# Batch-norm of pairwise outer products: statistics from 39x39 moment tables, W read from PSUM, and a tile loop split over three engines in a fixed order

## Chip, cores and metric

One core of one Trainium2 chip. The metric is device time in microseconds (us) of one launch. All runs below are fast-state runs. TensorE (PE) works only in the statistics (its last matmul ends at 102 us in the kernel before). The engines are called PE, DVE (VectorE), ACT (ScalarE), POOL (GpSimd) and SP (SyncE), as in the profile.

## The reference

Inputs xi and xj are 1024 x 39 x 16, f32. For each of the 741 pairs of fields (r, c) with c < r it forms the 16x16 outer product of xj[r] and xi[c], normalises it with the mean and variance of that pair over batch and both 16s, applies gamma and beta, and multiplies by a 16x16 matrix W.

```python
rows, cols = np.tril_indices(39, k=-1)                      # 741 pairs
cross = xj[:, rows, :, None] * xi[:, cols, None, :]         # 1024 x 741 x 16 x 16
mean = jnp.mean(cross, axis=(0, 2, 3), keepdims=True)
var = jnp.mean(jnp.square(cross - mean), axis=(0, 2, 3), keepdims=True)
normed = (cross - mean) * jax.lax.rsqrt(var + BN_EPS)
normed = normed * gamma[None, :, None, None] + beta[None, :, None, None]
out = normed[:, :, None, :, :] * W[None, None, :, :, :]
return jnp.transpose(out, (0, 2, 1, 3, 4))                  # 1024 x 1 x 741 x 16 x 16, 777 MB
```

So 5 MB are read and 777 MB written. Folded, it is (xj * (xi * s) + t) * W with one s and one t per pair.

## The kernel before

The batch is on the partitions, 8 samples on each. After the statistics, a loop goes over the rows r and over groups of nt samples. For each tile: POOL scales xi by s (xs), ACT forms the 16 products per sample (DVE those of rows up to 6), DVE does one fused (y + t) * W per pair, in place, and one store takes the tile out.

```python
rows = ctx.enter_context(tc.tile_pool(name="rows", bufs=4))
scaled = ctx.enter_context(tc.tile_pool(name="scaled", bufs=2))
for r in order:                                   # short and long rows in turn
    n0 = first[r]
    nt = max(n for n in (1, 2, 4, 8) if NT % n == 0 and (n == 1 or n * r < F))
    for t0 in range(0, NT, nt):
        xs = scaled.tile([P, nt, r, E], F32, tag="xs", ...)
        nc.gpsimd.tensor_tensor(xs, xi_sb[:, t0 : t0 + nt, 0:r, :],
            s_sb[:, :, n0 : n0 + r, :].to_broadcast([P, nt, r, E]), ALU.mult)          # L166
        y = rows.tile([P, nt, r, E, E], F32, tag="y", ...)
        for t in range(nt):
            # ... r <= 6: one nc.vector.tensor_tensor for all products (L175), else:
            for i in range(E):
                nc.scalar.activation(y[:, t, :, i, :], xs[:, t], AF.Copy,
                                     scale=xj_sb[:, t0 + t, r, i : i + 1])             # L183
        y2 = y.rearrange("p t n i j -> p t n (i j)")
        for c in range(r):
            nc.vector.scalar_tensor_tensor(y2[:, :, c, :], y2[:, :, c, :],
                t_sb[:, n0 + c : n0 + c + 1], w_sb.to_broadcast([P, nt, EE]),
                ALU.add, ALU.mult)                                                     # L191
        nc.sync.dma_start(out_v[:, t0 : t0 + nt, n0 * EE : (n0 + r) * EE], ...)
```

The statistics (cut) build 741-wide pair products on DVE and POOL (L100), average them over the batch with 128 matmuls against ones (L111), and finish with 741-wide steps.

Of the kernel before, what the change touches and what calls it, by code (L numbers as in the profile page):

```python
# [7 lines left out]
F32 = mybir.dt.float32  # L8
AF = mybir.ActivationFunctionType
ALU = mybir.AluOpType  # L10
AX = mybir.AxisListType

BN_EPS = 1e-5
# Rows of at most this many pairs have their outer products on VectorE, the longer ones on ScalarE.
VECTOR_ROW = 6


@with_exitstack
def tile_pair_outer_batchnorm(
# [9 lines left out]
    """out[b, 0, (r, c), i, j] = (xj[b, r, i] * xi[b, c, j] * s[r, c] + t[r, c]) * W[i, j] for c < r,  # L29
    with s = gamma * rsqrt(var + eps) and t = beta - mean * s.  # L30

    The batch lies on the partitions, b = p * NT + t. Mean and variance of a pair need only the
    mean and the variance over E of each field: with a = xj[b, r], b = xi[b, c],
      mean_ij(a_i b_j)           = A B
      mean_ij((a_i b_j - m) ** 2) = (A B - m) ** 2 + (A ** 2 + va) vb + va B ** 2
    (A, B the means and va, vb the variances of a and b), and only positive terms are summed.
    """
# [6 lines left out]
    H0 = (NP + 1) // 2  # L44
    halves = ((0, H0), (H0, NP))
# [6 lines left out]
    s_sb = cpool.tile([P, 1, NP, 1], F32, name="s_sb")  # L52
    t_sb = cpool.tile([P, NP], F32, name="t_sb")
# [10 lines left out]
    with tc.tile_pool(name="stat", bufs=1) as st, tc.tile_pool(  # L64
        name="dev", bufs=2
    ) as devp, tc.tile_pool(name="ps", bufs=1, space=bass.MemoryType.PSUM) as psp:
        g_sb = st.tile([P, NP], F32, name="g_sb")
        b_sb = st.tile([P, NP], F32, name="b_sb")
        nc.gpsimd.dma_start(w_sb[:, 0, :], w.rearrange("o i j -> (o i j)").partition_broadcast(P))
        nc.gpsimd.dma_start(g_sb, gamma.partition_broadcast(P))  # L70
        nc.gpsimd.dma_start(b_sb, beta.partition_broadcast(P))
        ones = st.tile([P, P], F32, name="ones")
        nc.gpsimd.memset(ones, 1.0 / NB)

        # mean and variance over E of each field, per sample
        ma = st.tile([P, NT, F, 1], F32, name="ma")
        mb = st.tile([P, NT, F, 1], F32, name="mb")
        va = st.tile([P, NT, F, 1], F32, name="va")
        vb = st.tile([P, NT, F, 1], F32, name="vb")
        for t0 in range(0, NT, TS):  # L80
            for x, m, v in ((xj_sb, ma, va), (xi_sb, mb, vb)):
                xs, ms, vs = x[:, t0 : t0 + TS], m[:, t0 : t0 + TS], v[:, t0 : t0 + TS]
                nc.vector.tensor_reduce(ms[:, :, :, 0], xs, AX.X, ALU.add)  # L83
                nc.vector.tensor_scalar_mul(ms, ms, 1.0 / E)
                dev = devp.tile([P, TS, F, E], F32, tag="dev", name="dev")
                nc.vector.tensor_tensor(dev, xs, ms.to_broadcast([P, TS, F, E]), ALU.subtract)  # L86
                nc.scalar.activation(dev, dev, AF.Square)  # L87
                nc.vector.tensor_reduce(vs[:, :, :, 0], dev, AX.X, ALU.add)  # L88
                nc.vector.tensor_scalar_mul(vs, vs, 1.0 / E)
        ma, mb, va, vb = (x[:, :, :, 0] for x in (ma, mb, va, vb))  # L90
        sa = st.tile([P, NT, F], F32, name="sa")
        sb = st.tile([P, NT, F], F32, name="sb")
        nc.vector.tensor_mul(sb, mb, mb)  # L93
        nc.vector.tensor_mul(sa, ma, ma)
        nc.vector.tensor_add(sa, sa, va)

        def pairs(engine, rows, cols, name):
            q = st.tile([P, NT, NP], F32, name=name)
            for r in range(1, F):
                engine.tensor_tensor(  # L100
                    q[:, :, first[r] : first[r] + r],
                    rows[:, :, r : r + 1].to_broadcast([P, NT, r]),
                    cols[:, :, 0:r],
                    ALU.mult,
                )
            return q

        def batch_mean(ps, qs, start, stop):
            for k, (q, t) in enumerate((q, t) for q in qs for t in range(NT)):
                for acc, (n0, n1) in zip(ps, halves):  # L110
                    nc.tensor.matmul(  # L111
                        acc[:, : n1 - n0],
                        ones,
                        q[:, t, n0:n1],
                        start=start and k == 0,
                        stop=stop and k == len(qs) * NT - 1,
                    )

        # mean over the batch, on every partition
        q_c = pairs(nc.gpsimd, va, sb, "q_c")  # L120
        q_a = pairs(nc.vector, ma, mb, "q_a")
        ps_m = [psp.tile([P, 512], F32, name=f"ps_m{h}") for h in range(2)]
        ps_v = [psp.tile([P, 512], F32, name=f"ps_v{h}") for h in range(2)]
        batch_mean(ps_m, [q_a], True, True)
        q_b = pairs(nc.vector, sa, vb, "q_b")
        batch_mean(ps_v, [q_b, q_c], True, False)
        mean = st.tile([P, 1, NP], F32, name="mean")
        for acc, (n0, n1) in zip(ps_m, halves):
            nc.scalar.copy(mean[:, 0, n0:n1], acc[:, : n1 - n0])  # L129
        for t in range(NT):  # L130
            nc.vector.tensor_sub(q_a[:, t], q_a[:, t], mean[:, 0])  # L131
            nc.scalar.activation(q_a[:, t], q_a[:, t], AF.Square)  # L132
        batch_mean(ps_v, [q_a], False, True)

        # rstd = 1 / sqrt(var + eps), with a Newton step behind the table's square root
        var = st.tile([P, NP], F32, name="var")
        for acc, (n0, n1) in zip(ps_v, halves):
            nc.vector.tensor_scalar_add(var[:, n0:n1], acc[:, : n1 - n0], BN_EPS)  # L138
        inv = st.tile([P, NP], F32, name="inv")
        nc.vector.reciprocal(inv, var)  # L140
        rstd = st.tile([P, NP], F32, name="rstd")
        nc.scalar.activation(rstd, inv, AF.Sqrt)  # L142
        nc.vector.tensor_mul(inv, var, rstd)
        nc.vector.tensor_mul(inv, inv, rstd)  # L144
        nc.vector.tensor_scalar(inv, inv, -0.5, 1.5, ALU.mult, ALU.add)
        nc.vector.tensor_mul(rstd, rstd, inv)  # L146

        s2 = s_sb[:, 0, :, 0]
        nc.vector.tensor_mul(s2, rstd, g_sb)
        nc.vector.tensor_mul(t_sb, mean[:, 0], s2)  # L150
        nc.vector.tensor_sub(t_sb, b_sb, t_sb)

    # short and long rows in turn, so that VectorE and ScalarE share the outer products evenly
    order = []
    for k in range(1, (F - 1) // 2 + 1):
        order += [k, F - k]
    assert sorted(order) == list(range(1, F))

    rows = ctx.enter_context(tc.tile_pool(name="rows", bufs=4))
    scaled = ctx.enter_context(tc.tile_pool(name="scaled", bufs=2))  # L160
    for r in order:
        n0 = first[r]
        nt = max(n for n in (1, 2, 4, 8) if NT % n == 0 and (n == 1 or n * r < F))
        for t0 in range(0, NT, nt):
            xs = scaled.tile([P, nt, r, E], F32, tag="xs", name=f"xs_{r}_{t0}")
            nc.gpsimd.tensor_tensor(  # L166
                xs,
                xi_sb[:, t0 : t0 + nt, 0:r, :],
                s_sb[:, :, n0 : n0 + r, :].to_broadcast([P, nt, r, E]),
                ALU.mult,  # L170
            )
            y = rows.tile([P, nt, r, E, E], F32, tag="y", name=f"y_{r}_{t0}")
            for t in range(nt):
                if r <= VECTOR_ROW:
                    nc.vector.tensor_tensor(  # L175
                        y[:, t],
                        xs[:, t].unsqueeze(2).to_broadcast([P, r, E, E]),
                        xj_sb[:, t0 + t, r : r + 1, :].unsqueeze(3).to_broadcast([P, r, E, E]),
                        ALU.mult,
                    )  # L180
                else:
                    for i in range(E):
                        nc.scalar.activation(  # L183
                            y[:, t, :, i, :],
                            xs[:, t],
                            AF.Copy,
                            scale=xj_sb[:, t0 + t, r, i : i + 1],
                        )
            y2 = y.rearrange("p t n i j -> p t n (i j)")
            for c in range(r):  # L190
                nc.vector.scalar_tensor_tensor(  # L191
                    y2[:, :, c, :],
# [38 lines left out]
```

## Time and profile before

| | before |
|---|---|
| time, median | 3103.07 us (3102.97 to 3104.05, 3 runs) |
| DVE / ACT / POOL busy | 79% / 65% / 54% |
| share of the 16 DMA engines' time | 59% |
| statistics end (first scaling of the loop) | 112.5 us |

From the page of the kernel before, the three groups of the loop: line, engine, operation, tiles, a shape, count, then busy us, mean ns of one, and the idle time just before them with what ended most of it.

```profile
L191 DVE SCALAR_TENSOR_TENSOR y<-y,t_sb,w_sb 128x256 f32<-128x256 f32 (+2 forms) x5068 | 2314.6, 534 | 610.3 <-ACT y L183 610.1
L183 ACT ACTIVATE y<-xs,xj_sb 128x608 f32<-128x608 f32 (+31 forms) x4096 | 1994.9, 580 | 978.7 <-POOL xs L166 978.7
L166 POOL TENSOR_TENSOR xs<-xi_sb,s_sb 128x576 f32<-128x576 f32 (+19 forms) x206 | 1637.3, 7958 | 1368.8 <-ACT y L183 1315.6
```

The odd number is the 7958 ns in the third line: the same engine does a multiply of 352 elements in 0.79 us elsewhere in this trace.

### The profile page before, as it was taken

What the parts mean: (1) busy time and instruction counts of PE and PEld (TensorE: products, weight loads), DVE (VectorE), ACT (ScalarE), POOL (GpSimd) and SP (SyncE); (2) the same over time, 40 slices, a digit from 0 to 9 for tenths busy, and PEclk for the clock granted to TensorE, in tenths of its full rate; (3) what the DMA queues carried; (4) which work ended last, traced back from release to release, by engine and by line L of the source; (5) the groups of instructions that cost most, each with busy time, mean ns of one, the idle gap of its engine ahead of it and who ended that gap; (6) DMA issues with size and microseconds to landing.
All of it is one profiled execution on the core that took longest, in us unless ns stands there. A gap on an engine that the chain in (4) does not pass through costs nothing.

```text
span 3100.0 us, 10969 instructions
## 1 busy us (share of the span) xinstructions
PE 45.6 (1%) x128; PEld 26.7 (1%) x128; DVE 2448.0 (79%) x5253; ACT 2015.7 (65%) x4117; POOL 1659.1 (54%) x252
## 2 busy tenths in 40 slices
PE   2300000000000000000000000000000000000000
PEld 1100000000000000000000000000000000000000
DVE  8687888888888787777777787768777777778786
ACT  2446455464635777777676767676868686868685
POOL 2375757665666656555646464646363636362623
PEclk9655555555555555555555555555555555555555
DMA  2165656566555656666656656565656565666666
GB/s 78 78 265 228 282 244 259 250 269 271 250 252 248 293 237 281 256 268 268 288 249 263 265 240 272 246 281 242 270 243 281 244 281 249 276 263 268 275 267 275
DMA packets 43653, 783.71 MB, mean 253 GB/s; under 512 B 3472, under 2 KB 4496, under 8 KB 11824
## 3 DMA queue, kind: packets, MB, share of 16 engines
q1 hardware_dynamic: 42784, 779.56, 59.1%
q10 hardware_dynamic: 576, 2.56, 0.2%
q0 software_dynamic: 208, 0.89, 0.1%
q14 instruction: 84, 0.69, 0.1%
q8 instruction: 1, 0.02, 0.0%
HBM read 6.00 MB, written 776.99 MB: 253 GB/s over the span
## 4 chain that ended last, share of the span: by engine, by line
ACT 48%; POOL 45%; DVE 3%; issue 2%; PE 1%; DMA 0%; POOLq 0%; DVEq 0%; ACTq 0%
ACT y L183 48%; POOL xs L166 45%; PE ps_v L111 1%; DVE y L191 1%; DVE q_a L100 1%; DVE dev L86 0%; PE ps_m L111 0%; DMA xj_sb<-in_r_xj_dram 0%; DVE ma L83 0%; DVE vb L88 0%; DVE va L88 0%; DVE mb L83 0%; DVE inv L140 0%; DVE rstd L146 0%; DVE inv L144 0%
## 5 line engine op out<-in xcount | busy, mean ns | idle before, releaser
L191 DVE SCALAR_TENSOR_TENSOR y<-y,t_sb,w_sb 128x256 f32<-128x256 f32 (+2 forms) x5068 | 2314.6, 534 | 610.3 <-ACT y L183 610.1
L183 ACT ACTIVATE y<-xs,xj_sb 128x608 f32<-128x608 f32 (+31 forms) x4096 | 1994.9, 580 | 978.7 <-POOL xs L166 978.7
L166 POOL TENSOR_TENSOR xs<-xi_sb,s_sb 128x576 f32<-128x576 f32 (+19 forms) x206 | 1637.3, 7958 | 1368.8 <-ACT y L183 1315.6
L175 DVE TENSOR_TENSOR y<-xs,xj_sb 128x256 f32<-128x256 f32 (+5 forms) x48 | 51.5, 1136 | 1.5 <-POOL xs L166 1.4
L100 POOL TENSOR_TENSOR q_c<-va,sb 128x8 f32<-128x8 f32 (+37 forms) x38 | 19.6, 553 | 39.3 <-DVE sb L93 39.3
L87 ACT ACTIVATE dev<-dev 128x1248 f32<-128x1248 f32 x8 | 9.9, 1243 | 26.1 <-DVE dev L86 25.9
L129 ACT COPY mean<-ps_m 128x371 f32<-128x371 f32 (+1 forms) x2 | 0.9, 468 | 31.0 <-PE ps_m L111 31.0
L138 DVE TENSOR_SCALAR var<-ps_v 128x371 f32<-128x371 f32 (+1 forms) x2 | 1.1, 545 | 22.1 <-PE ps_v L111 22.0
L100 DVE TENSOR_TENSOR q_a<-ma,mb 128x8 f32<-128x8 f32 (+37 forms) x38 | 18.2, 554 | 0.0
L142 ACT ACTIVATE rstd<-inv 128x741 f32<-128x741 f32 x1 | 0.8, 822 | 25.9 <-DVE inv L140 25.9
L111 PE MATMUL ps_m<-q_a,ones 128*128 128x371 f32 (+1 forms) x32 | 15.7, 662 | 56.1 <-DVE q_a L100 56.1
L83 DVE TENSOR_REDUCE ma<-xj_sb 128x78 f32<-128x1248 f32 x4 | 5.8, 1452 | 6.9 <-DMA xj_sb<-in_r_xj_dram 6.9
L111 PE MATMUL ps_v<-q_a,ones 128*128 128x371 f32 (+1 forms) x32 | 10.2, 474 | 0.0
L111 PE MATMUL ps_v<-q_b,ones 128*128 128x371 f32 (+1 forms) x32 | 10.2, 474 | 0.0
L111 PE MATMUL ps_v<-q_c,ones 128*128 128x371 f32 (+1 forms) x32 | 10.1, 474 | 0.0
L100 DVE TENSOR_TENSOR q_b<-sa,vb 128x8 f32<-128x8 f32 (+37 forms) x38 | 9.9, 341 | 0.0
L111 PEld LDWEIGHTS ps_m<-q_a,ones 128*128 128x128 f32 x32 | 8.5, 274 | 62.7 <-issue 57.0
L131 DVE TENSOR_TENSOR q_a<-q_a,mean 128x741 f32<-128x741 f32 x8 | 6.8, 925 | 1.6 <-ACT mean L129 1.6
L132 ACT ACTIVATE q_a<-q_a 128x741 f32<-128x741 f32 x8 | 6.6, 822 | 1.1 <-DVE q_a L131 1.0
L111 PEld LDWEIGHTS ps_v<-q_a,ones 128*128 128x128 f32 x32 | 6.1, 189 | 3.9
L111 PEld LDWEIGHTS ps_v<-q_c,ones 128*128 128x128 f32 x32 | 6.1, 189 | 3.9
L111 PEld LDWEIGHTS ps_v<-q_b,ones 128*128 128x128 f32 x32 | 6.1, 189 | 3.9
(30 smaller groups left out, 49.6 us busy)
## 6 DMA issues: line engine op xcount, KB each, us to landing
out_dram<-y SPq DMA_DIRECT2D x14, 4608.0 KB, 12.4
out_dram<-y SPq DMA_DIRECT2D x15, 4096.0 KB, 11.2
out_dram<-y SPq DMA_DIRECT2D x12, 4864.0 KB, 12.9
out_dram<-y SPq DMA_DIRECT2D x12, 4352.0 KB, 11.8
out_dram<-y SPq DMA_DIRECT2D x14, 3584.0 KB, 10.0
out_dram<-y SPq DMA_DIRECT2D x15, 3072.0 KB, 8.8
out_dram<-y SPq DMA_DIRECT2D x12, 3840.0 KB, 10.6
out_dram<-y SPq DMA_DIRECT2D x12, 3328.0 KB, 9.3
```

What stands on the lines that cost most here:

```text
L83: nc.vector.tensor_reduce(ms[:, :, :, 0], xs, AX.X, ALU.add)
L87: nc.scalar.activation(dev, dev, AF.Square)
L100: engine.tensor_tensor(q[:, :, first[r] : first[r] + r], rows[:, :, r : r + 1].to_broadcast([P, NT, r]), cols[:, :, 0:r], ALU.mult,)
L111: nc.tensor.matmul(acc[:, : n1 - n0], ones, q[:, t, n0:n1], start=start and k == 0, stop=stop and k == len(qs) * NT - 1,)
L129: nc.scalar.copy(mean[:, 0, n0:n1], acc[:, : n1 - n0])
L131: nc.vector.tensor_sub(q_a[:, t], q_a[:, t], mean[:, 0])
L132: nc.scalar.activation(q_a[:, t], q_a[:, t], AF.Square)
L138: nc.vector.tensor_scalar_add(var[:, n0:n1], acc[:, : n1 - n0], BN_EPS)
L166: nc.gpsimd.tensor_tensor(xs, xi_sb[:, t0 : t0 + nt, 0:r, :], s_sb[:, :, n0 : n0 + r, :].to_broadcast([P, nt, r, E]), ALU.mult,)
L175: nc.vector.tensor_tensor(y[:, t], xs[:, t].unsqueeze(2).to_broadcast([P, r, E, E]), xj_sb[:, t0 + t, r : r + 1, :].unsqueeze(3).to_broadc ...
L183: nc.scalar.activation(y[:, t, :, i, :], xs[:, t], AF.Copy, scale=xj_sb[:, t0 + t, r, i : i + 1],)
L191: nc.vector.scalar_tensor_tensor(y2[:, :, c, :], y2[:, :, c, :], t_sb[:, n0 + c : n0 + c + 1], w_sb.to_broadcast([P, nt, EE]), ALU.add, AL ...
```

## The change

It has four parts. (1) The statistics come from moments: shifted sums and squares per sample, 48 small matmuls into 39x39 tables, and seven spreads back to 128 partitions. Gamma and beta are loaded row by row into such tables. (2) W gets a second copy in PSUM, and DVE reads that one. (3) For rows over 6, POOL takes 4 of 16 products and 13% of the pairs. (4) Tiles are about twice as large with two buffers instead of four, stores are cut into parts, and the instruction order is written down instead of left to the scheduler. The rows now go from 6 up to 38 and then from 5 down to 1, instead of short and long in turn.

```diff
+UNITS = 76
+POOL_I = 4
+POOL_SHARE = 0.13
 # statistics, cut
-        nc.gpsimd.dma_start(b_sb, beta.partition_broadcast(P))
+        for r in range(1, F):
+            nc.sync.dma_start(g_sq[r : r + 1, 0:r], gamma[n0 : n0 + r].unsqueeze(0))
+            nc.scalar.dma_start(b_sq[r : r + 1, 0:r], beta[n0 : n0 + r].unsqueeze(0))
 # ... sums, shifts, squares (POOL and DVE subtract, ACT squares, DVE reduces), gram, 39-wide steps ...
+        for r0, r1 in ROW_GROUPS:          # s and t of 6 rows to all partitions
+            nc.vector.tensor_tensor(wide, stq..., eye[:, r0:r1]..., ALU.mult)
+            nc.tensor.matmul(ps..., ones[0:F, :], wide..., start=True, stop=True)           # L226
+            for r in range(r0, r1):
+                nc.scalar.copy(st_sb[:, :, first[r] : first[r] + r], ps[:, r - r0, :, 0:r]) # L234
 # loop
+    w_dve = wpsp.tile([P, 1, EE], F32, name="w_dve")        # in PSUM
+    nc.scalar.copy(w_dve, w_sb)
+        return max(n for n in (1, 2, 4, 8) if NT % n == 0 and (n == 1 or n * r <= UNITS))
+    order = list(range(VECTOR_ROW, F)) + list(range(VECTOR_ROW - 1, 0, -1))
-    rows = ctx.enter_context(tc.tile_pool(name="rows", bufs=4))
+    rows = ctx.enter_context(tc.tile_pool(name="rows", bufs=2))
+                if i < E - POOL_I:
+                    nc.scalar.activation(y[:, t, :, i, :], xs[:, t], AF.Copy, scale=scale)  # L282
+                else:
+                    nc.gpsimd.tensor_scalar(y[:, t, :, i, :], xs[:, t], scale, 1.0, ...)    # L284
+        split = r - (int(r * POOL_SHARE + 0.5) if r > VECTOR_ROW else 0)
+        step = max(1, 16 // nt)
+        # pairs c < split on DVE, with a store of nt samples after every `step` of them:
-                    w_sb.to_broadcast([P, nt, EE]),
+                w_dve.to_broadcast([P, nt, EE]),                                            # L297
+        # pairs from split on: POOL adds t pair by pair (L313), multiplies by w_sb at once (L317)
+    with tc.manual_schedule():
+        scale_xi(0); products(0); scale_xi(1)
+        for k in range(len(tiles)):
+            finish(k); products(k + 1); scale_xi(k + 2)      # bounds checks cut
```

## The prediction

> **What bounds the kernel now.** I read the page's busy shares, then the chain that ended last, then the list of who waited for whom, and last the timeline of a few stretches of the loop. The page first: no engine and no queue is near full.
>
> ```profile
> PE 45.6 (1%) x128; PEld 26.7 (1%) x128; DVE 2448.0 (79%) x5253; ACT 2015.7 (65%) x4117; POOL 1659.1 (54%) x252
> q1 hardware_dynamic: 42784, 779.56, 59.1%
> ACT 48%; POOL 45%; DVE 3%; issue 2%; PE 1%; DMA 0%; POOLq 0%; DVEq 0%; ACTq 0%
> ```
>
> The third line is the chain: ACT and POOL in turn, though POOL is only 54% busy and DVE, at 79%, is hardly on it. The waits (total, times, longest) say the same; each of ACT and POOL waits for the other:
>
> ```profile
> POOL xs L166 <- ACT y L183: 1315.6, 148, 17.5
> ACT y L183 <- POOL xs L166: 978.7, 56, 28.9
> DVE y L191 <- ACT y L183: 610.1, 87, 15.3
> ```
>
> The timeline names the fault. Columns are start, length, engine, line, operation. Two scalings of xi of the same shape on POOL, the second with DVE idle:
>
> ```profile
> 1677.85 22.24 POOL L166 TENSOR_TENSOR xs<-xi_sb,s_sb 128x352 f32<-128x352 f32 x1 [8.14 <-ACT y L183]
> ...
> 1700.05 0.79 POOL L166 TENSOR_TENSOR xs<-xi_sb,s_sb 128x352 f32<-128x352 f32 x1
> ```
>
> In between DVE ran its fused add-multiply back to back, from before the first one until it ended:
>
> ```profile
> 1668.58 30.87 DVE L191 SCALAR_TENSOR_TENSOR y<-y,t_sb,w_sb 128x256 f32<-128x256 f32 x69 [10.16 <-ACT y L183]
> ```
>
> So a 0.79 us job takes 22 us whenever DVE has a run of line 191 under way. All 206 scalings hold 94,848 elements per partition; undisturbed ones fit 0.18 us + 1.71 ns per element (352: 0.78; 608: 1.22 in single records), so they are worth 199 us and take 1637. ACT has two tiles of slack at most, runs dry, and then DVE runs dry.
>
> [...] stores of 4864 KB land in 12.9 us and of 2688 KB in 7.8, a difference of 437 GB/s.
>
> **The change part by part.**
> *Statistics.* The first POOL scaling of the loop starts at 112.5 us now. Out go 114 small pair products (DVE 28, POOL 20 us), 128 matmuls and the 741-wide passes. In come eight matmul triples and 39-wide steps. But gamma and beta are now 38 one-row loads each, and beta's sit on ACT's queue ahead of its first activation. In the compiled order a load waits for the one four places ahead on the same queue, the first four for the input loads, which land by 19 us before and perhaps 17 now. With 2 us per round of four (estimate: the shortest stores show 1.3 us fixed[...]) ACT is free at about 17 + 34/4 x 2 = 34 us. Then POOL's five subtractions (2.3 us each by the fit), the last square and reduce by about 49, small steps to 58, and 38 narrow copies out of PSUM (0.2 us each) to about 68. Gain: about 46 us.
> *POOL's stall.* w goes to PSUM for DVE, so line 191's successor has one SBUF input. [...] xs falls from 1637 to about 180 us of busy time.
> *Work moved.* For rows over 6 POOL takes 4 of 16 products and about 13% of the pairs. Totals over the loop, instructions times start-to-start time of undisturbed ones in the trace: ACT 3072 x (0.186 us + 0.84 ns per element) = 1500 us; DVE 2208 fused instructions, 256 to 2048 wide, at (elements/0.96 ns + 129 ns; 512 wide takes 662)[...], with the short rows' products, about 1795; POOL 181 xs + 500 products + 572 pairs = 1253.
> *Stores.* One per tile becomes four to six. A contiguous run of n KB occupies one of 16 DMA engines for 10.5 + 37.6 n ns (packet records: 48 ns for 1 KB, 163 for 4, 314 for 8). Longest runs are now 2 to 8 KB, so the stores' total rises from 1830 to 1894 us. So DMA becomes the busiest resource.
> *The two buffers.* Tiles double in size and y has two buffers instead of four. The order lets ACT and POOL write tile k+2 only when every store of tile k has landed, and DVE can start a tile only when all its products are there. Let A be ACT's time for a tile, D DVE's, M its stores'. Then the tile's round trip is R = A + D + tail + 1.6 us (DVE end to first packet 0.9, last packet to ACT's start 0.7), where the tail is what stores are still owed when DVE ends; two tiles share one R. Per tile the time is the largest of M, A, D and R/2, seen four ways:
> - row 7, 8 samples: A 26.9, D 13.8, M 19.6: ACT.
> - row 22, 2 samples: A 11.6, D 13.3, M 13.9, tail about 7: R/2 = 33.5/2 = 16.7.
> - row 30: A 14.1, D 18.1, M 18.9, tail 8: R/2 = 20.9.
> - row 38: A 16.7, D 23.0, M 23.9, tail 8.5: R/2 = 24.9.
>
> So M, R/2 and D lie within 20% of each other, and the wait for the buffer decides. I carried the recurrence by arithmetic over all 105 tiles: rows 6-9 take 127 us, 10-19 444, 20-27 556, 28-34 596, 35-38 386, and rows 5 to 1, which DVE does alone (71 us of work, partly beside the last stores), 66. Sum 2175, with 68 for the statistics: about 2240.
>
> **The rivals.**
> 1. *DMA alone is the bound*: 68 + 1894 + about 40 of filling and emptying = 2000 us. For it: the store total is the largest sum. Against it: with two buffers the queue runs empty while a tile is remade; that costs about 240 us in my sum. Three buffers in the same recurrence give 2000.
> 2. *The stall stays*, because the pointer scalar still comes from SBUF and counts as a second input. Then DVE's 1795 and POOL's 1253 exclude each other: about 3000 us plus statistics, no gain. Against it: [...] the division of labour makes sense only if the stall is gone.
> 3. *POOL is slower than estimated.* At 1.5 times its figures the sum doesn't move (2244); at twice it becomes the bound, near 2650. For it: the new forms are unmeasured.
> 4. *Sustained stores are slower than bursts.* The queue has so far had pauses; the best 77 us slice moved 293 GB/s. 10% slower: 2315[...].
>
> **Range and chances.** [...] the statistics are good for 20 us either way; rivals 3 and 4 point up, rival 1 down. 2240, with 2100 to 2390 for 8 in 10. Faster by over 2%: 0.96; within 2%: 0.02; slower: 0.02.
>
> **What would show the steps right or wrong.** Right: POOL's xs near 0.9 us for 352 elements to 2.3 for 1216, whatever DVE does; [...] ACT's waits mostly for DMA (the buffer), not for POOL; DMA share 85 to 90% in the loop; a period near 33 us for two tiles of row 22; first loop activation near 68 us. Wrong: xs above 5 us (rival 2), DMA share at 97% (rival 1), POOL over 85% busy and DVE waiting for it (rival 3), 1 KB to 8 KB packets longer than 48 to 314 ns (rival 4). The prediction fails if the wait for the stores is shorter than a whole tile's, for instance because products of one part may start before the last store has landed.

The sum it came to is 2240 us, and one term of that sum is cut: a fixed cost for DVE's operand in PSUM on each of the 2208 fused instructions, 77 of DVE's 1795 us and 26 of the 2240 (2214 without it). D, R/2 and the times of the rows, as printed, contain it.

Three more things were not shown then. That W in PSUM ends POOL's stall was an assumption; e1 and e2 test it. POOL's 500 us of products and the additions in its 572 of pairs are estimates, made from the fit of the trace: 0.18 us + 0.86 ns per element, half of its 1.71, for operations with one input (later measured: 0.84 ns). And of the fixed times, the trace of the kernel before shows 0.89 us in the median from DVE's end to a store's first packet, and 1.19 us beside the packets for 185 stores that ran alone (1.3 in the text); the 0.7 us after the last packet and the 2 us per round of four loads were estimates (in the changed kernel 0.42 to 0.75 us, where the store queue stood idle, and 1.44 us: one load of beta every 0.36). DVE's elements/0.96 ns + 129 ns is a fit of the trace (256, 512 and 1024 wide: 396, 663 and 1196 ns from start to start in the median). The "whenever" is too strong: in the kernel before, 56 of the 147 scalings that began in a run of DVE were held up by over 6 us (e9).

## The result, and the profile after

The changed kernel takes **2239.32 us** (median; 2239.08 to 2239.36, 4 runs) against 3103.19 us of the kernel before (4 runs). The ratio is 0.7216 (0.7206 to 0.7226). Here and below a ratio is the mean time of one kernel's fast runs over the mean of the other's in the same rounds, so it is not quite the ratio of the medians quoted. The prediction was 2240.

The page of the changed kernel: busy us and share of each engine, then the DMA engines' busy tenths in 40 slices, then the store queue (packets, MB, share of 16 engines).

```profile
PE 18.7 (1%) x70; PEld 11.9 (1%) x70; DVE 1758.6 (79%) x2314; ACT 1523.6 (68%) x3127; POOL 1428.4 (64%) x1572
...
DMA  2377888889998888989898999999999999999987
...
q1 hardware_dynamic: 170924, 779.58, 86.8%
```

DVE is again at 79%, but of a span 862 us shorter. The resource that is now busiest is DMA. Its groups, in the same columns as before:

```profile
L297 DVE SCALAR_TENSOR_TENSOR y<-y,st_sb,w_dve 128x512 f32<-128x512 f32 (+2 forms) x2208 | 1665.5, 835 | 442.4 <-issue 410.4
L282 ACT ACTIVATE y<-xs,xj_sb 128x112 f32<-128x112 f32 (+31 forms) x3072 | 1505.4, 586 | 559.4 <-DMA out_dram<-y 349.6
L313 POOL TENSOR_SCALAR y<-y,st_sb 128x512 f32<-128x512 f32 (+2 forms) x331 | 243.0, 752 | 599.6 <-ACT y L282 599.6
L284 POOL TENSOR_SCALAR y<-xs,xj_sb 128x112 f32<-128x112 f32 (+31 forms) x1024 | 569.9, 581 | 61.8 <-DMA out_dram<-y 55.7
L317 POOL TENSOR_TENSOR y<-y,w_sb 128x2048 f32<-128x2048 f32 (+3 forms) x99 | 425.7, 4300 | 8.3
L256 POOL TENSOR_TENSOR xs<-xi_sb,st_sb 128x768 f32<-128x768 f32 (+20 forms) x105 | 182.3, 1736 | 75.2 <-DVE y L272 58.1
```

The scalings of xi hold the same elements as before and take 182.3 us instead of 1637.3. ACT no longer waits for POOL's xs; what ends most of its idle time is a store, which frees a buffer. The list of waits of the changed kernel (total us, times, longest):

```profile
DVE y L297 <- issue: 410.4, 94, 24.4
ACT y L282 <- DMA out_dram<-y: 349.6, 62, 16.6
ACT y L282 <- issue: 134.0, 20, 8.1
```

"issue" stands for a wait whose releaser the profile doesn't show, so look at where it sits. The timeline of the changed kernel in row 22 (start, length, engine, line, operation; in brackets the idle time before):

```profile
788.67 12.60 DVE L297 SCALAR_TENSOR_TENSOR y<-y,st_sb,w_dve 128x512 f32<-128x512 f32 x19 [6.83 <-issue]
...
802.54 12.60 DVE L297 SCALAR_TENSOR_TENSOR y<-y,st_sb,w_dve 128x512 f32<-128x512 f32 x19 [1.27 <-issue]
...
809.94 4.30 POOL L284 TENSOR_SCALAR y<-xs,xj_sb 128x352 f32<-128x352 f32 x8 [1.77 <-DMA out_dram<-y]
810.02 11.63 ACT L282 ACTIVATE y<-xs,xj_sb 128x352 f32<-128x352 f32 x24 [7.56 <-issue]
814.21 1.44 POOL L256 TENSOR_TENSOR xs<-xi_sb,st_sb 128x736 f32<-128x736 f32 x1
821.74 12.60 DVE L297 SCALAR_TENSOR_TENSOR y<-y,st_sb,w_dve 128x512 f32<-128x512 f32 x19 [6.59 <-issue]
...
843.90 6.53 ACT L282 ACTIVATE y<-xs,xj_sb 128x368 f32<-128x368 f32 x13 [8.07 <-issue]
```

This is the round trip of one buffer. ACT starts at 810.02, together with POOL, whose record names the store as releaser. ACT ends at 810.02 + 11.63 = 821.65, and DVE starts 0.09 us later, so DVE's "issue" is a wait for the tile's products. DVE ends at 834.34; ACT gets the buffer back at 843.90, after the stores still owed have landed. From 788.67 to 821.74 two tiles pass: 33.07 us. The scaling at 814.21 (736 elements, 1.44 us) is an undisturbed one by the prediction's fit.

The table of stretches of the changed kernel (stretch, us, then busy us with counts of PE, PEld, DVE, ACT, POOL, then clock, DMA share, GB/s):

```profile
640.00:1200.00 560.00, 0.00 (x0) 0.00 (x0) 430.80 (x652) 390.05 (x768) 370.06 (x421) 0.50 0.87 355
...
1790.00:2170.00 380.00, 0.00 (x0) 0.00 (x0) 336.02 (x503) 244.58 (x360) 258.66 (x227) 0.50 0.98 404
```

In the middle of the loop the DMA engines pause 13% of the time. In the last long rows they are full, at 98%. The prediction had named 97% as a sign for its rival 1, that DMA alone is the bound; the experiments come back to this.

### The profile page after: what moved, and what is told of

Its sections match the earlier page's. It is cut to its first block, busy times and chain, and to the rows that moved or that the text cites. A ratio compares the mean times of both kernels' runs of the same rounds, so it can differ in the third digit from the quotient of the medians.

```text
span 2237.6 us, 9393 instructions
## 1 busy us (share of the span) xinstructions
PE 18.7 (1%) x70; PEld 11.9 (1%) x70; DVE 1758.6 (79%) x2314; ACT 1523.6 (68%) x3127; POOL 1428.4 (64%) x1572
## 3 DMA queue, kind: packets, MB, share of 16 engines
q1 hardware_dynamic: 170924, 779.58, 86.8%
## 5 line engine op out<-in xcount | busy, mean ns | idle before, releaser
L297 DVE SCALAR_TENSOR_TENSOR y<-y,st_sb,w_dve 128x512 f32<-128x512 f32 (+2 forms) x2208 | 1665.5, 835 | 442.4 <-issue 410.4
L282 ACT ACTIVATE y<-xs,xj_sb 128x112 f32<-128x112 f32 (+31 forms) x3072 | 1505.4, 586 | 559.4 <-DMA out_dram<-y 349.6
L313 POOL TENSOR_SCALAR y<-y,st_sb 128x512 f32<-128x512 f32 (+2 forms) x331 | 243.0, 752 | 599.6 <-ACT y L282 599.6
L284 POOL TENSOR_SCALAR y<-xs,xj_sb 128x112 f32<-128x112 f32 (+31 forms) x1024 | 569.9, 581 | 61.8 <-DMA out_dram<-y 55.7
L317 POOL TENSOR_TENSOR y<-y,w_sb 128x2048 f32<-128x2048 f32 (+3 forms) x99 | 425.7, 4300 | 8.3
L256 POOL TENSOR_TENSOR xs<-xi_sb,st_sb 128x768 f32<-128x768 f32 (+20 forms) x105 | 182.3, 1736 | 75.2 <-DVE y L272 58.1
L272 DVE TENSOR_TENSOR y<-xs,xj_sb 128x1536 f32<-128x1536 f32 (+5 forms) x48 | 48.8, 1092 | 3.4 <-PE ps L226 3.4
L133 POOL TENSOR_TENSOR dev<-xj_sb,shift 128x1248 f32<-128x1248 f32 x4 | 9.3, 2327 | 36.1 <-ACT shift_r L127 28.4
L226 PE MATMUL ps<-wide,ones 39*128 39x468 f32 (+1 forms) x14 | 10.2, 921 | 5.7 <-DVE wide L219 5.7
L156 PE MATMUL ps_g<-fb,fa 128*39 128x79 f32 x32 | 5.9, 339 | 40.0 <-DVE fb L142 40.0
L107 DVE TENSOR_REDUCE total<-xi_sb 128x78 f32<-128x1248 f32 x4 | 5.8, 1444 | 0.0
```

The source lines that it names most:

```text
L107: nc.vector.tensor_reduce(total[:, t0 : t0 + TS, x], src[:, t0 : t0 + TS], AX.X, ALU.add)
L133: engine.tensor_tensor(dev, src[:, t0 : t0 + TS], shift[:, x : x + 1, :].unsqueeze(3).to_broadcast([P, TS, F, E]), ALU.subtract,)
L226: nc.tensor.matmul(ps.rearrange("p r x f -> p (r x f)"), ones[0:F, :], wide.rearrange("p r f -> p (r f)"), start=True, stop=True,)
L256: nc.gpsimd.tensor_tensor(xs, xi_sb[:, t0 : t0 + nt, 0:r, :], s_sb[:, :, n0 : n0 + r, :].to_broadcast([P, nt, r, E]), ALU.mult,)
L272: nc.vector.tensor_tensor(y[:, t], xs[:, t].unsqueeze(2).to_broadcast([P, r, E, E]), xj_sb[:, t0 + t, r : r + 1, :].unsqueeze(3).to_broadc ...
L282: nc.scalar.activation(y[:, t, :, i, :], xs[:, t], AF.Copy, scale=scale)
```

## The experiments

Twelve kernels ran, four each on one chip with its own runs of the kernel before (medians 3100.5, 3100.8 and 3101.3 us). All gave right results, except one.

| run | median us | ratio to before |
|---|---|---|
| after | 2239.32 | 0.7216 |
| e1_w_in_sbuf | 2915.33 | 0.9402 |
| e2_before_w_in_psum | 2413.48 | 0.7783 |
| e3_before_new_stats | 3064.28 | 0.9882 |
| e4_no_pool_share | 2486.68 | 0.8019 |
| e5_small_tiles | 2526.07 | 0.8147 |
| e6_small_tiles_3_buffers | 2118.92 | 0.6833 |
| e7_finer_stores | 2174.68 | 0.7013 |
| e8_scheduler_order | 2287.80 | 0.7378 |
| e9_w_in_sbuf_narrow | 3149.15 | 1.0154 |
| e10_beta_loads_on_sp | 2222.74 | 0.7167 |
| e11_all | 2045.69 | 0.6596 |
| e12_half_the_stores (wrong) | 2004.21 | 0.6462 |

The theory: W in PSUM frees POOL, and that is most of the gain; after it, the wait for one of two buffers bounds the loop. The rivals: the gain comes from the better division and order of the work, and PSUM is incidental; or the stores' own time is the bound already.

### e1: the changed kernel with W read from SBUF again

```diff
-                w_dve.to_broadcast([P, nt, EE]),
+                w_sb.to_broadcast([P, nt, EE]),
```

> The changed kernel, with DVE reading w from SBUF again instead of PSUM; all else kept. Theory[...]: while a run of DVE's fused instruction is under way POOL's reads stall, so DVE's 1705 us and POOL's about 1400 us of the loop lie one after the other: about 3100 us in all, POOL's xs of 1216 elements well over 10 us in the mean against 2.27, and DVE's 512-wide instruction unchanged at about 0.66 us start to start when undisturbed. Rival (larger tiles, the fixed order and the division of work give the gain): at most 2350 us.

2915.33 us, 676 us over the changed kernel. So the rival, that PSUM is incidental, falls. But the size is not the full exclusion that my theory expected, and the scalings of xi did not stretch as it said: those of 1216 elements took 2.41 us in the mean. From the page of this run:

```profile
PE 18.7 (1%) x70; PEld 11.9 (0%) x70; DVE 2682.6 (92%) x2314; ACT 1520.7 (52%) x3127; POOL 2291.2 (79%) x1572
...
L297 DVE SCALAR_TENSOR_TENSOR y<-y,st_sb,w_sb 128x512 f32<-128x512 f32 (+2 forms) x2208 | 2589.5, 1248 | 194.2 <-POOL y L284 172.7
...
L284 POOL TENSOR_SCALAR y<-xs,xj_sb 128x112 f32<-128x112 f32 (+31 forms) x1024 | 1177.9, 1171 | 353.7 <-DMA out_dram<-y 331.5
```

Both sides pay: DVE's fused instructions take 924 us more (2589.5 - 1665.5) and POOL's products 608 more (1177.9 - 569.9). The timeline of this run shows how:

```profile
998.61 41.67 DVE L297 SCALAR_TENSOR_TENSOR y<-y,st_sb,w_sb 128x512 f32<-128x512 f32 x38
1004.79 8.24 POOL L284 TENSOR_SCALAR y<-xs,xj_sb 128x368 f32<-128x368 f32 x8 [2.83 <-DMA out_dram<-y]
```

38 fused instructions in 41.67 us are 1.10 us each, and 8 products in 8.24 us are 1.03 each. With W in PSUM they take 0.66 (12.60 us for 19 in the changed kernel) and 0.55 (4.41 for 8 of this width). So here the two engines take turns, one instruction each, instead of POOL waiting for a whole run of DVE.

### e2: the kernel before with W in PSUM, and nothing else

```diff
+    w_dve = wpsp.tile([P, 1, EE], F32, name="w_dve")   # pool in PSUM
+    nc.scalar.copy(w_dve, w_sb)
...
-                    w_sb.to_broadcast([P, nt, EE]),
+                    w_dve.to_broadcast([P, nt, EE]),
```

> The kernel before, with one thing changed: w copied to PSUM once and read from there by DVE. Theory: xs falls from 1637 us busy to about 200, ACT's waits for POOL vanish, and DVE becomes the bound with 5068 fused instructions worth 2237 us plus 51 us of products: about 2430 us (115 us of statistics before it, some emptying after it), 2380 to 2520. Rival (the loop's structure is what held it): above 2900 us.

2413.48 us: one operand moved gives 687 of the 864 us. From the page of this run:

```profile
PE 44.7 (2%) x128; PEld 25.9 (1%) x128; DVE 2347.8 (97%) x5253; ACT 2017.2 (84%) x4118; POOL 226.9 (9%) x252
...
L170 POOL TENSOR_TENSOR xs<-xi_sb,s_sb 128x576 f32<-128x576 f32 (+19 forms) x206 | 205.0, 996 | 2108.8 <-ACT y L187 1863.2
```

The same 206 scalings take 205.0 us instead of 1637.3, and the bound becomes DVE itself, 97% busy. This also tells what the rest of the change is for: with POOL free, DVE and ACT have to be relieved to get further, and POOL, at 9%, can do it.

### e3: the kernel before with the new statistics only

```diff
 # the statistics block of the kernel before is replaced by that of the changed kernel; the loop is kept
```

> The kernel before with only the statistics of the changed one. Theory: the loop starts at about 75 us instead of 112.5 and is otherwise as before: 3066 us, ratio 0.988. Rival (the earlier start is lost in the loop, which waits for something else): within 0.3% of before.

3064.28 us, 36 us less. The statistics are worth what the earlier start of the loop says and no more.

### e4: the changed kernel without POOL's share

```diff
-POOL_I = 4
-POOL_SHARE = 0.13
+POOL_I = 0
+POOL_SHARE = 0.0
```

> The changed kernel with POOL doing only the scaling of xi: all 16 products on ACT, all pairs on DVE. Theory (two buffers make the round trip A + D + tail the limit): ACT 2000 us, DVE 1947, stores unchanged at about 1905: the recurrence with the measured durations gives 2484 us; 2430 to 2540. Rival (DMA alone is the bound of the changed kernel): ACT at 2000 still fits beside the stores for most rows, so within 3% of 2239, at most 2300 us.

2486.68 us. Moving work to POOL is worth 247 us, though neither ACT (81% busy in this run) nor DVE (80%) is full without it. This speaks for the round trip: A and D are terms of it, so shortening them pays even where no engine is full. Without POOL's share this kernel, with its new statistics, is even 73 us behind e2, which has four smaller buffers (and the old order of rows, so this pair does not isolate the buffers).

### e5 and e6: smaller tiles, with two and with three buffers

```diff
-UNITS = 76
+UNITS = 50
```

and for e6 in addition

```diff
-    rows = ctx.enter_context(tc.tile_pool(name="rows", bufs=2))
+    rows = ctx.enter_context(tc.tile_pool(name="rows", bufs=3))
```

> The changed kernel with tiles of at most 50 pair-samples instead of 76, still two buffers (rows over 25 go one sample at a time). Half of what is needed to tell buffers from DMA; compare with the next. Theory (two buffers, round trip A + D + tail): the fixed costs of each instruction and tile weigh more, the recurrence with measured durations gives 2501 us (DVE's total 1912, ACT 1500, stores 1891). Rival (DMA bound): stores are no more than before, so at most 2280.

> The same small tiles with three buffers of y instead of two. Theory: the wait for the stores of the tile two back goes, DVE (1912) and DMA (1891) are left as bounds: the recurrence gives 2118 us, that is 380 us less than with two buffers and 5% less than the changed kernel; ACT's waits for DMA fall to a small part. Rival (DMA bound): as the run with two buffers, within 2%.

2526.07 and 2118.92 us. The work of the two is the same; one more buffer is worth 407 us. The waits of e5:

```profile
ACT y L282 <- DMA out_dram<-y: 701.9, 134, 23.2
...
DVE y L297 <- issue: 478.1, 145, 10.1
```

and of e6:

```profile
ACT y L282 <- DMA out_dram<-y: 355.3, 116, 8.9
DVE y L297 <- issue: 102.8, 54, 9.6
```

ACT's wait for stores only halves, which I had not expected; I had put it at a small part. The stretches of e6 tell why. From 560 to 1050 us (rows 20 to 27) the DMA engines are 99% busy and DVE works 452 of 490 us: there the stores themselves are about full. From 1050 to 2040 us (rows 28 to 38) DVE works without a pause, so ACT's wait hits nobody. Over the run DVE's own wait falls from 478 to 103 us, and it is 93% busy. The wait to judge by is that of the engine behind, not that of ACT.

### e7: stores half as large

```diff
-        step = max(1, 16 // nt)
+        step = max(1, 8 // nt)
```

> The changed kernel with stores of half as many pairs (8 over the samples of a tile instead of 16). Theory: the tail that is still owed when DVE ends gets shorter, though the stores cost more in total (1992 against 1917 us by the packet times): the recurrence gives 2164 us. Rival (DMA bound): the store total rises by 75 us and the time with it, 2290 to 2320.

2174.68 us, 65 us less, though the stores then cost more: the page gives

```profile
q1 hardware_dynamic: 286556, 779.60, 93.5%
```

which is 93.5% of 2172.1 us = 2031 us against 86.8% of 2237.6 us = 1942 us. A rise of 89 us in transfer time beside a fall of 65 us in the total cannot be had if the store total is the bound. A store issued earlier leaves less owed when DVE ends, which is the tail of the round trip. Where the time went tells more: to DVE's last end, rows 10 to 19 take 9 us less, rows 20 to 27 35, rows 28 to 34 20, and rows 35 to 38 0.5. In this run the DMA share of rows 28 to 38 is 1.02 (the times of packets can overlap, so a share near 1 is no proof of a bound by itself).

### e8: the order left to the scheduler

```diff
-    with tc.manual_schedule():
+    if True:
```

> The changed kernel with the loop's order left to the scheduler instead of fixed. The compiled order differs mainly on POOL (a scaling or the next tile's products come ahead of the multiply by w) and in the order of stores. Theory: the same buffers and the same work, so the same limit: within 3% of 2239, more likely slower, as POOL's pairs come later. Rival (the fixed order is a large part of the gain): above 2350.

2287.80 us: the fixed order is worth 48 us, 2% of the changed kernel.

### e9: W in SBUF, narrow tiles, four buffers

e1 left a question: why did a POOL instruction wait up to 38 us in the kernel before and mostly only one turn in e1? This run gives the changed kernel the tile widths of the kernel before.

```diff
-UNITS = 76
+UNITS = 38
...
-    rows = ctx.enter_context(tc.tile_pool(name="rows", bufs=2))
+    rows = ctx.enter_context(tc.tile_pool(name="rows", bufs=4))
...
-                w_dve.to_broadcast([P, nt, EE]),
+                w_sb.to_broadcast([P, nt, EE]),
```

> The changed kernel with w in SBUF for DVE, as in the first experiment, but with tiles of at most 38 pair-samples and four buffers, so that DVE's instructions of rows 20 and up are 256 wide instead of 512. Asked: why POOL waited out whole runs of DVE in the kernel before (22 us), and took turns with it one for one in the first experiment. Theory (the width of DVE's instruction decides): POOL instructions that start within a 256-wide run wait for its end, 5 to 13 us for single instructions in rows 20 to 38, and almost none do in the rows below 20. Rival (it is POOL's operation that decides, the two-input scaling starves and the one-input products do not): turns one for one in all rows, no product over 2 us. Time for either: 2900 to 3300 us.

3149.15 us (2 runs), and neither theory was right by itself: most of the loop goes in turns, and some instructions starve. Two groups of four products in the timeline of this run:

```profile
1023.67 2.86 POOL L284 TENSOR_SCALAR y<-xs,xj_sb 128x368 f32<-128x368 f32 x4
...
1034.93 21.64 POOL L284 TENSOR_SCALAR y<-xs,xj_sb 128x368 f32<-128x368 f32 x4 [3.68 <-DMA out_dram<-y]
```

The first follows other POOL work without a gap. The second comes after 3.68 us of idling and takes 21.64 us. I sorted all POOL instructions that began while DVE ran fused instructions back to back with W in SBUF, in three kernels that have them (before, e1, e9). Of 2,586 that began within 60 ns of the one before, the longest took 3.2 us. Of 625 that began after a longer pause, 98 took over 6 us more than undisturbed ones: 56 of 147 in the kernel before, where they make 1444 of the 1637 us, 15 of 201 in e1, 27 of 277 here. With W in PSUM (the changed kernel and e2) none of 1,685 did. So what starves is an instruction that comes after a pause into a DVE run under way. In the kernel before, 147 of the 206 scalings come so. Why only some of them starve stays open; width alone does not decide it.

### e10: beta's loads on SP's queue

```diff
-            nc.scalar.dma_start(b_sq[r : r + 1, 0:r], beta[n0 : n0 + r].unsqueeze(0))
+            nc.sync.dma_start(b_sq[r : r + 1, 0:r], beta[n0 : n0 + r].unsqueeze(0))
```

> The changed kernel with beta's 38 row loads issued from SP beside gamma's, so that ACT has no loads ahead of its first activation. Theory: ACT's shift comes at about 13 us instead of 30.7, the rest of the statistics then runs into the input loads and DVE's own work, the loop starts at about 61 instead of 75 us: 2225 us, ratio to the changed kernel 0.994. Rival (SP's longer queue of 76 loads, eight at a time, becomes the wait): no gain or a loss, the statistics then waiting for beta at their end.

2222.74 us, 17 us less by the medians and 15 by the ratios. In the changed kernel's timeline ACT's first activation stands at 30.70, behind 38 loads issued from its queue; in the timeline of this run:

```profile
12.47 0.24 ACT L124 ACTIVATE shift<-ps_s 128x78 f32<-128x78 f32 x1 [8.15 <-PE ps_s L113]
```

Eighteen microseconds earlier, and most of it reaches the end.

### e11: what helped, together

```diff
-UNITS = 76
+UNITS = 50
-POOL_SHARE = 0.13
+POOL_SHARE = 0.18
-            nc.scalar.dma_start(b_sq[r : r + 1, 0:r], beta[n0 : n0 + r].unsqueeze(0))
+            nc.sync.dma_start(b_sq[r : r + 1, 0:r], beta[n0 : n0 + r].unsqueeze(0))
-    rows = ctx.enter_context(tc.tile_pool(name="rows", bufs=2))
+    rows = ctx.enter_context(tc.tile_pool(name="rows", bufs=3))
```

> A version meant to beat both: tiles of at most 50 pair-samples with three buffers, POOL's share of the pairs 0.18 instead of 0.13, beta's loads on SP. By the recurrence with measured durations: DVE 1808 us, POOL 1757, ACT 1500, stores 1888; 2045 us, 2020 to 2080. If the larger share makes POOL the bound instead, above 2119.

**2045.69 us** (5 runs, 2045.55 to 2046.13), the fastest that gives right results: 34% below the kernel before and 8.6% below the changed one. From its page and its table of stretches:

```profile
PE 18.7 (1%) x70; PEld 11.9 (1%) x70; DVE 1854.2 (91%) x3757; ACT 1527.3 (75%) x3127; POOL 1779.6 (87%) x2179
```

```profile
400.00:1600.00 1200.00, 0.00 (x0) 0.00 (x0) 1127.57 (x2432) 944.72 (x1773) 1131.89 (x1358) 1.00 0.99 410
1600.00:2000.00 400.00, 0.00 (x0) 0.00 (x0) 399.93 (x962) 245.42 (x360) 329.08 (x381) 1.00 0.95 395
```

From 400 to 1600 us the DMA engines are 99% busy, and after that DVE is (399.93 of 400 us). DVE and POOL work 94% of the first stretch, so the stores are about full there, though not alone. In the changed kernel's middle (87%) they are not.

### e12: half of each store left out

Wrong: only the first half of the samples of each store is written.

```diff
-                out_v[:, t0 : t0 + nt, (n0 + c0) * EE : (n0 + c1) * EE],
-                y[:, :, c0:c1, :].rearrange("p t n e -> p t (n e)"),
+                out_v[:, t0 : t0 + nt // 2, (n0 + c0) * EE : (n0 + c1) * EE],
+                y[:, 0 : nt // 2, c0:c1, :].rearrange("p t n e -> p t (n e)"),
```

> The changed kernel storing only the first half of the samples of each tile; the result is wrong on purpose (the other half is never written). Theory (round trip A + D + tail): halving the stores takes 958 us of transfer away but shortens only the tail, the recurrence gives 1993 us. Rival (DMA alone is the bound): the bound falls to DVE's 1705 us, about 1830 us with statistics and emptying.

2004.21 us (2 runs). From its page:

```profile
q1 hardware_dynamic: 89516, 391.09, 48.8%
```

48.8% of 2002.5 us is 977 us of transfer, 965 less than in the changed kernel, and the time falls by only 235. What remains is A + D and the fixed handoffs of the round trip, the short rows and the statistics. In rows 35 to 38 half the transfer takes 36 of 379 us away, and DVE's pauses there fall from 45 us to 10.

## Why the prediction was right

**What bounds the kernel before: shown.** e2 changes one operand of one instruction and removes the stall: 1637 to 205 us of scalings, 687 us of time. The prediction read this from one 22.24 us record beside one of 0.79 us.

**POOL's stall goes: right.** About 180 us were foretold for xs and 182.3 were measured. What I believed about the stall itself was too strong. POOL is not shut out for as long as DVE runs; it mostly gets every second turn (e1: 1.10 us per fused instruction beside 1.03 per product), and starves only when it comes after a pause, and then not always (56 of 147 in the kernel before, e9). The prediction for the changed kernel did not depend on this, only on the assumption that W in PSUM ends the stall, which the changed kernel and e2 then showed (none of 1,685 POOL instructions took over 6 us more; the count is under e9). The rival "the stall stays, about 3000 us plus statistics" did: e1, which is that case, measured 2915.

**DVE's operand in PSUM: a term that was wrong.** I put a fixed cost on each of the 2208 fused instructions. No trace showed one. In the changed kernel those of 512 elements start every 658 ns; in the kernel before, undisturbed, every 662. So the cost is none, and the sum without the term, 2214, was the better one at this step.

**Work moved: POOL mis-sized, without effect on the time.** In the loop DVE came to 1714 us (1795 foretold; 77 of the difference is the term above), ACT to 1506 (1500), POOL to 1412 (1253). Two terms of POOL missed by about as much. The products came to 570 us where 500 were foretold: the slope was near the estimate (0.84 ns per element, estimated 0.86), the fixed part is 0.25 to 0.27 us and not 0.18. The pairs came to 669 where 572 were foretold, mostly by the in-place multiply by W: 4.52 us for 2048 elements, 2.11 ns per element + 0.19 us, where I used 1.71. POOL has pauses, so the 13% excess went into them, as the prediction said of rival 3.

**Stores: 2% to 3% low.** Packets of 1, 2, 4 and 8 KB took 48, 88, 165 and 317 ns in the mean; the prediction's fit gives 48, 86, 161 and 311. The queue's total rose from 59.1% of 3100.0 to 86.8% of 2237.6, that is from 1832 to 1942 us, where 1894 were foretold. Rival 4 (sustained stores are slower than bursts) falls too: 404 GB/s over 380 us, with packets about as long as before.

**The two buffers: right for most of the loop, and this carried the number.** Two tiles of row 22 take 33.07 us, foretold near 33. The bands can be compared at the end of DVE's last tile in each. (The prediction's text cut them where the last store lands, so its first figure, 127, and its last, 66, stand here as 115 and 71, out of the same recurrence.)

| stretch, to DVE's last end | prediction's recurrence, us | measured, us |
|---|---|---|
| start of the loop | 68 | 75 |
| rows 6 to 9 | 115 | 113 |
| rows 10 to 19 | 445 | 448 |
| rows 20 to 27 | 559 | 559 |
| rows 28 to 34 | 596 | 588 |
| rows 35 to 38 | 384 | 379 |
| rows 5 to 1 | 71 | 69 |

e5, e6, e7 and e12 confirm it from four sides: another buffer pays 407 us at the same work, a shorter tail pays 65 in spite of dearer transfers, and half the transfer pays a quarter of what it saves. The recurrence with the changed kernel's durations forecast e4, e5, e6, e7, e11 and e12, before they ran, within 1% (e5: 2501 us against 2526 is the worst).

Rows 35 to 38 are the exception, 379 us of the loop. The prediction put R/2 (24.9 us for a tile of row 38) above M (23.9) and D (23.0); the period measured is 24.1 to 24.6 us, with the DMA engines 98% busy. There e7's shorter tail takes 0.5 us away, against 20 and 35 in the two stretches before. So in these rows the stores' own time is about the limit, as rival 1 has it, or at least cannot be told from the round trip.

**Statistics: start at 75 instead of 68.** The wait of ACT behind beta's loads was foretold (34 us; 30.7 measured). The end was not. I had the last square and reduce done by about 49 us; it ended at 57.1, and that is the term that missed. The small steps after it (49 to 58 foretold, 57.1 to 64.7 measured) and the last step (58 to 68 foretold, 64.7 to 75.3 measured) were sized about right, though it is the 14 matmuls that set the last step's pace and not the 38 copies (10.2 us busy against 4.2). From the timeline of the kernel before, where its loop begins:

```profile
112.51 3.01 POOL L166 TENSOR_TENSOR xs<-xi_sb,s_sb 128x128 f32<-128x128 f32 x2 [50.37 <-DVE s_sb L149]
```

and from that of the changed kernel:

```profile
29.41 1.28 ACT L124 ACT_TABLE_LOAD   x1 [29.41 <-DMA b_sq<-in_L_rec_beta_dram]
30.70 0.24 ACT L124 ACTIVATE shift<-ps_s 128x78 f32<-128x78 f32 x1
...
31.13 2.35 DVE L144 SCALAR_TENSOR_TENSOR fb<-total,shift 128x78 f32<-128x78 f32 x1
...
55.69 1.45 DVE L142 TENSOR_REDUCE fb<-dev 128x78 f32<-128x1248 f32 x1 [1.37 <-ACT dev L140]
...
64.67 10.24 PE L226 MATMUL ps<-wide,ones 39*128 39x468 f32 x14 [5.67 <-DVE wide L219]
...
75.32 26.97 ACT L282 ACTIVATE y<-xs,xj_sb 128x112 f32<-128x112 f32 x96
```

The 14 matmuls take 10.24 us. The 31.13 line shows the old fault in small, with DVE as the one held: a 78-element fused instruction of DVE, both inputs in SBUF, takes 2.35 us instead of 0.23 beside POOL's subtraction (2.36 us in the trace). Three in a row do so, and DVE comes to its reduces only at 38.56 us; POOL's next subtraction then waits 3.5 us for one of them. This is likely a good part of the 8 us, but no run tested it.

**How close is luck in part.** With the measured durations and start put into the same recurrence (PSUM cost none, POOL's real costs, 75 us), it gives 2223, so it is some 16 us low of the 2239 measured. A PSUM term too high by some 26 us met statistics 7 us too short and stores and handoffs some 16 us too low. The mechanism held; an agreement within 1 us was not earned.

**Where the 864 us come from.** Each measured by itself: W in PSUM 687, the statistics 36. The rest, 141 us, is the other parts jointly, and they cannot be added up singly: on top of PSUM, POOL's share is worth 247 and the fixed order 48, and two buffers cost part of it again (e6, with three and smaller tiles, is 120 us faster than the changed kernel). The new order of rows was not varied by any run.

## What to carry to other kernels

When a small job on POOL now and then takes ten times its usual length (here 22.24 us instead of 0.79), look at what DVE runs at that moment, and try one of DVE's two SBUF inputs in PSUM before dividing the work anew (here that took the scalings from 1637 to 205 us, e2). When no engine and no queue is full, write down the round trip of one buffer (produce, finish, drain, hand back) and divide it by the number of buffers: here it told what a further buffer (407 us, e6 against e5), an earlier store (65, e7) or relieving an engine (247, e4) pays, before anything was run. And a sum that hits within 1 us still deserves a check term by term.
